# Projections in tiles of 32 columns, and one PSUM accumulator for both halves of an LSTM step

## The chip, the cores and the metric

The kernel runs on one core of one Trainium2 chip. The metric is the device time of one execution in microseconds (us). TensorE multiplies matrices and writes its results to PSUM; VectorE (DVE in the profile) and ScalarE (ACT) read them there. GpSimd (POOL) and SyncE (SP) issue loads and do a little preparation.

## The reference

Four residual layers run over x of shape (4, 1024, 512), each reading the sum so far. Cut to what matters:

```python
x = x + rnn(x)     # h = tanh(x_t @ Wx + b + h @ Wh)
x = x + ssm(x)     # conv of 4 taps, proj @ Wp, u = x @ Ws, a scan over time, y @ Wo + bo
x = x + lstm(x)    # A = x_t @ Wx + b + h @ Wh; i,f,o = sigmoid; g = tanh
                   # c = f*c + i*g; h = o*tanh(c)
x = x + adapt(x)   # x @ (base + rank-8 update), per batch row
```

The RNN and the LSTM are sequential: 1024 steps, each of which needs the h of the step before. Batch is 4, so a step multiplies only 4 rows of h by a 512 x 512 (RNN) or 512 x 2048 (LSTM) matrix.

## The kernel before

**Chunks and passes.** Time is cut into 32 chunks of 32 steps (slots). A pass `do_pass(c)` runs the LSTM on chunk c, the RNN on chunk c+2, the state-space layer for chunk c+1 and the adapter layer for chunk c-1, so that four layers are under way at once. Passes -2 and -1 are a prologue without LSTM; passes 1 to 24 are in a loop unrolled 12 times. Order on every engine is the order in which the program is written (`manual_schedule`); the framework puts in the semaphore waits. In a slot the order is: all LSTM matmuls; a job for TensorE, if the slot has one; the RNN matmuls; then the work of VectorE and ScalarE.

**A step of the LSTM.** h is held in float32 and split into three bf16 parts (`split`, line 203), so that 4 batch rows times 3 parts make 12 stationary columns. TensorE is used as four tiles of 32 columns (`CT = 32`): tile j takes the same 12 columns of h and a quarter of the outputs, and writes to PSUM partitions 32j and up. The outputs are worked on in two halves, A and B (`mh` = 0 and 1), 256 columns for each tile: 64 for each of four gates. Each half has its own accumulator, `acc2[0]` and `acc2[1]`, each in a PSUM bank of its own. The contraction runs over four chunks k of h; half A makes the chunks 0 and 1 of the new h, half B the chunks 2 and 3. A matmul at line 365 covers one k, one bf16 part of the weights, one tile and one half: 4 x 3 x 4 x 2 = 96 of 256 columns. They are ordered A (k = 0, 1), B (k = 0), A (k = 2, 3), B (k = 1, 2, 3), so that A's sums are complete after 60.

**What follows the matmuls.** `Half` holds it: `transpose` (line 382) reads the half's accumulator from PSUM, `sum` (387) adds the bf16 parts and the input projection, `gates` (394) is tanh on ScalarE, then `products` (398), `cell` (403), `tanh` (408), `h` (411) and two `split` (203). A and B are interleaved in an order written out by hand: A's transpose, A's sum, B's transpose, A's gates, A's products, and so on. `rnn_mm` (340), `rnn_pre` (348, 349) and `rnn_h` (352) are the RNN's step.

**Projections.** They are matrix products over a whole chunk (128 tokens), placed in slots by `jobs`: the taps of the state-space layer (437) in slots 1 to 4, `skip` (444) in slot 5, its output (493) in slot 13, and `project2` (329), the LSTM's input, in slots 15 to 30. These four use the array with 128, 64 or 128 stationary columns at once. `project0` (315), the RNN's input in slots 0 and 10 to 12, already runs as four tiles of 32. The adapter's matmuls (678) run in slots 6 to 9. Results of projections are moved out of PSUM at line 304. The tile `pb` holds the taps' result in `pb[:, 0]` and the skip result in `pb[:, 1]`, both in one bank; ScalarE reads the first at lines 461, 462 and 465.

**Loads.** `wx2` (4 MB) comes in four pieces through the buffer `xw2[0]`, and POOL copies each into its columns' order (line 173). `wo` comes in four DMAs.

Of the kernel before, what the change touches and what calls it, by code (L numbers as in the profile page):

```python
# [8 lines left out]
F32 = mybir.dt.float32  # L9
# [29 lines left out]
def cond_resid_kernel(ctx: ExitStack, tc: tile.TileContext, a: dict, out: bass.AP):  # L39
# [117 lines left out]
    wp = const.tile([P, TAPS, KC, 2 * NS], F32, name="wp", tag="wp")  # L157
    quads(nc.sync, wp[:, TAPS - 1], a["Wp"].rearrange("(j c q) n -> j q c n", j=4, c=KC))
    ws = load_rows(const, "ws", a["Ws"], NS, nc.sync)

    wo = const.tile([NS, D], F32, name="wo", tag="wo")
    for c in range(KC):
        nc.sync.dma_start(
            out=wo[:, P * c : P * (c + 1)].rearrange("p (j q) -> p j q", j=4),
            in_=a["Wo"].rearrange("p (j c q) -> p j c q", j=4, c=KC)[:, :, c],
        )
    wx2 = const.tile([P, KC, 4 * D], F32, name="wx2", tag="wx2")
    come = xw2[0].rearrange("p g c t b -> p (g c t b)")
    for k in range(KC):
        quads(nc.sync, come, a["Wx2"].rearrange("(j c q) n -> j q c n", j=4, c=KC)[:, :, k])  # L170
        for g in range(4):
            cols = slice(g * D, (g + 1) * D)
            nc.gpsimd.tensor_copy(
                wx2[:, k, cols].rearrange("p (c j q) -> p c j q", c=KC, j=4),
                come[:, cols].rearrange("p (j c q) -> p c j q", j=4, c=KC),
            )
    w1 = layer[:, 1]

    base = layer[:, B - 1]
# [17 lines left out]
    def upper(x):  # L197

        return x.bitcast(BF16)[..., 1::2]
# [17 lines left out]
    nc.vector.memset(s1, 0.0)  # L217

    acc0 = psum.tile([P, P], F32, name="acc0", tag="acc0")
    acc2 = [psum.tile([P, 2 * P], F32, name=f"acc2{i}", tag=f"acc2{i}") for i in range(2)]  # L220
    for t in (acc0, *acc2):
        nc.vector.memset(t, 0.0)

    def softplus_parts(dst, z, n, tag, cut=1):
# [75 lines left out]
    def bank(name, shape, tag="fill", bufs=2):  # L300
        return psum.tile(shape, F32, name=name, tag=tag, bufs=bufs)

    def evacuate(dst, ps, bias, scale):
        nc.scalar.activation(dst.rearrange("p t b -> p (t b)"), ps, AF.Identity, bias=bias, scale=scale)  # L304

    def project0(c, m):

        ps = bank("proj0", [P, TOK])

        def mm():  # L310

            for k in range(KC):
                for j in range(4):
                    n0 = P * j + CT * m
                    nc.tensor.matmul(  # L315
                        ps[CT * j : CT * (j + 1), :], wx0[:, k, n0 : n0 + CT], xin[c % XBUFS][:, k],
                        start=(k == 0), stop=(k == KC - 1),
                    )

        return mm, lambda: evacuate(xw0[c % 2][:, m], ps, b0[:, 0, m : m + 1], 1.0)  # L320

    def project2(c, g, m):

        ps = bank("proj2", [P, TOK])
        n0 = g * D + P * m

        def mm():
            for k in range(KC):
                nc.tensor.matmul(  # L329
                    ps, wx2[:, k, n0 : n0 + P], x2[c % 2][:, k], start=(k == 0), stop=(k == KC - 1)  # L330
                )

        return mm, lambda: evacuate(xw2[c % 2][:, g, m], ps, b2s[:, g, m : m + 1], 1.0 if g == 3 else 0.5)


    def rnn_mm(c, t):
# [15 lines left out]
        nc.scalar.activation(h0[c % 2][:, :, t, :], pre0[t % 2], AF.Tanh)  # L352


    def lstm_mm(c, t, kh, mh, ks=(0, 1)):


        h = h2[c % 2] if t else h2[(c - 1) % 2]
        for k in (2 * kh + x for x in ks):
            parts = upper(h[:, k, (t - 1) % TC].rearrange("p s b -> p (s b)"))  # L360
            for n in range(NP):
                w = wh2[n][:, k].rearrange("p (g n) -> p g n", g=4)
                for j in range(4):
                    n0 = P * j + 2 * CT * mh
                    nc.tensor.matmul(  # L365
                        acc2[mh][CT * j : CT * j + NP * B, :], parts, w[:, :, n0 : n0 + 2 * CT],
                        start=(k == 0 and n == 0), stop=(k == KC - 1 and n == NP - 1),
                    )

    def lstm_input(c, t, m):  # L370
        nc.scalar.copy(tt2[m][t % 2][:, :, :, :B], xw2[c % 2][:, :, 2 * m : 2 * m + 2, t, :])  # L371
# [1 line left out]
    class Half:  # L373
# [6 lines left out]

        def transpose(self):
            nc.vector.transpose(  # L382
                self.tt[:, :, :, B:].rearrange("p g c b -> p (g c) b"), acc2[self.m]
            )

        def sum(self):
# [34 lines left out]
    def ssm_jobs(c):  # L421
        x, h, po = xin[c % XBUFS], h0[c % 2], {}
        v, act = nc.vector, nc.scalar

        def sm(name):
            return small.tile([NS, TOK], F32, name=name, tag=name, bufs=1)

        jobs = [
            (m // 2, ("gap", "end")[m % 2], lambda m=m: v.tensor_add(x1[:, m, 3:, :], x[:, m], h[:, m]))
            for m in range(KC)  # L430
        ]
        pb = bank("pb", [P, 2, TOK], tag="pb", bufs=1)


        def taps(k):
            for tap in range(TAPS):
                nc.tensor.matmul(  # L437
                    pb[:, 0, :], wp[:, tap, k], x1[:, k, tap : tap + TC, :],
                    start=(tap == 0 and k == 0), stop=(tap == TAPS - 1 and k == KC - 1),
                )  # L440

        def skip():
            for k in range(KC):
                nc.tensor.matmul(  # L444
                    pb[:NS, 1, :], ws[:, k], x1[:, k, 3:, :], start=(k == 0), stop=(k == KC - 1)
                )

        cg, z, e, u, w, p = (sm(n) for n in ("cg", "z", "e", "u", "w", "p"))
        bt, vv, y = z, e, w
        v3, y3 = (t.rearrange("p (t b) -> p t b", b=B) for t in (vv, y))  # L450
        y_last = y3[:, TC - 1, :]
        jobs += [(1 + k, "pe", lambda k=k: taps(k)) for k in range(KC)]
        jobs.append((5, "pe", skip))

        def turn(n):
            cols = slice(n * TOK // 4, (n + 1) * TOK // 4)
            v.reciprocal(u[:, cols], u[:, cols])


        jobs += [  # L460
            (4, "end", lambda: act.activation(z, pb[:NS, 0, :], AF.Identity, bias=vec[:NS, 0:1])),
            (4, "end", lambda: act.activation(e, pb[:NS, 0, :], AF.Abs, bias=vec[:NS, 0:1])),
            (5, "end", lambda: act.activation(e, e, AF.Exp, scale=-1.0)),
            (5, "end", lambda: act.activation(u, e, AF.Copy, bias=2.0)),
            (6, "end", lambda: act.activation(cg, pb[NS:, 0, :], AF.Tanh, bias=vec[NS:, 0:1])),
            (7, "end", lambda: v.tensor_mul(u, u, e)),
            (7, "end", lambda: v.tensor_mul(w, u, u)),
            (7, "end", lambda: act.activation(p, w, AF.Copy, scale=2.0 * SERIES[-1])),
            (12, "end", lambda: act.copy(s1, y_last)),
        ]  # L470

        chain = [lambda q=q: v.scalar_tensor_tensor(p, p, 2.0 * q, w, ALU.add, ALU.mult) for q in SERIES[-2::-1]]
        chain += [
            lambda: v.scalar_tensor_tensor(p, p, 2.0, u, ALU.add, ALU.mult),
            lambda: v.scalar_tensor_tensor(bt, z, 0.0, p, ALU.max, ALU.add),
            lambda: v.scalar_tensor_tensor(vv, pb[:NS, 1, :], vec[:NS, 1:2], bt, ALU.add, ALU.mult),
        ]
        for b in range(B):
            chain.append(lambda b=b: v.tensor_tensor_scan(
                y3[:, :, b], decay, v3[:, :, b], s1[:, b : b + 1], ALU.mult, ALU.add  # L480
            ))

        chain += [
            lambda: v.scalar_tensor_tensor(y, y, dt, cg, ALU.mult, ALU.mult),
        ]
        place = lambda n: ("gap", "end", "end")[n % 3]
        jobs += [(6 + n // 3, place(n), lambda n=n: turn(n)) for n in range(4)]
        jobs += [(8 + n // 3, place(n), f) for n, f in enumerate(chain)]

        def out_mm():  # L490
            po[0] = bank("ssm_out", [P, KC, TOK], tag="po", bufs=1)
            for m in range(KC):
                nc.tensor.matmul(po[0][:, m, :], wo[:, P * m : P * (m + 1)], y, start=True, stop=True)  # L493

        def x2_end(m):
            v.scalar_tensor_tensor(
                x2[c % 2][:, m].rearrange("p t b -> p (t b)"), po[0][:, m, :], bo[:, 0, m : m + 1],
                x1[:, m, 3:, :].rearrange("p t b -> p (t b)"), ALU.add, ALU.add,
            )

        jobs += [
            (13, "pe", out_mm),
            *((13 + m // 2, "end", lambda m=m: x2_end(m)) for m in range(KC)),
            (14, "end", lambda: act.copy(x1[:, :, 0:3, :], x1[:, :, TC : TC + 3, :])),
        ]
        return jobs
# [187 lines left out]
    def do_pass(c, src=None, dst=None, lstm=True, rnn=True, ssm=True, last=False):  # L694
# [23 lines left out]
        for t in range(TC):  # L718
            if lstm:
                A, Bh = Half(c, t, 0), Half(c, t, 1)  # L720
                lstm_mm(c, t, 0, 0)
                lstm_mm(c, t, 0, 1, (0,))
                lstm_mm(c, t, 1, 0)
                lstm_mm(c, t, 0, 1, (1,))
                lstm_mm(c, t, 1, 1)
            do(t, "pe")
            if rnn:
                rnn_mm(c + 2, t)
# [119 lines left out]
```

## Time and profile before

| What | Value |
|---|---|
| Median of 3 runs | 5007.96 us (5005.07 to 5009.45) |
| Profiled execution, its own time | 5000.53 us |
| Its span | 4998.8 us, TensorE clock 0.987 of full |
| TensorE matmuls busy | 4776.3 us, 96% |
| VectorE busy | 3728.2 us, 75% |
| L365, LSTM matmuls | 98304, 2877.8 us busy |
| L340, RNN matmuls | 32768, 1106.6 us busy |
| L329, `project2` matmuls | 4096, 593.3 us busy |
| L315, `project0` matmuls | 4096, 137.2 us busy |
| L382, LSTM transposes on VectorE | 2048 of 450 ns |

A float32 matmul appears as two records, so counts at L329 and L315 are twice those of the program. PE is TensorE's matmul, PEld its weight load, which overlaps. A line of a group reads: line, engine, operation, out<-in by name, shapes, count | busy us, mean ns of one | idle time of the engine before it and what ended it. In the timeline a line has its start, its duration and, in brackets, the idle time of that engine before it. Busy time counts overlapping matmuls once.

### The profile page before, as it was taken

The page shows a single profiled execution, that of the slowest core. Times are in us where ns is not written, and L with a number is a line of the kernel's source. Part 1 is how long each engine was busy: PE and PEld are TensorE (multiplying, and loading weights), DVE is VectorE, ACT ScalarE, POOL GpSimd, SP SyncE. Part 2 cuts the span into 40 slices and gives each one's busy share as a digit, 9 for nine tenths or more (in the row PEclk, how much of TensorE's full clock was granted, in tenths as well). Part 3 has the DMA queues.
Part 4 walks back from the last instruction along what each step waited for, and adds up shares of the span by engine and source line. Part 5 has one row for each costly group of instructions (what it writes and reads, how often), then busy time and mean ns, then how long its engine had stood idle before and what let it go on. Part 6 is the DMA issues. An engine that isn't in the chain of part 4 may idle for free.

```text
span 4998.8 us, 313167 instructions
## 1 busy us (share of the span) xinstructions
PE 4776.3 (96%) x142944; PEld 4156.1 (83%) x142944; DVE 3728.2 (75%) x17652; ACT 1617.2 (32%) x8135; POOL 62.9 (1%) x110
## 2 busy tenths in 40 slices
PE   5899999999999999999999999999999999999976
PEld 3778888888888888888888888888888888888864
DVE  3577777777777777777777777777777777777766
ACT  2223333333333333333333333333333333333322
POOL 3000000000000000000000000000000000000000
PEclk6999999999999999999999999999999999999999
DMA  5210000000000000000000000000000000000000
GB/s 130 92 38 8 8 6 8 6 8 8 8 8 6 6 8 8 8 9 6 8 6 9 8 9 8 6 6 8 9 8 8 6 7 7 8 6 6 4 5 7
DMA packets 39957, 66.97 MB, mean 13 GB/s; under 512 B 10321, under 2 KB 27345, under 8 KB 37601
## 3 DMA queue, kind: packets, MB, share of 16 engines
q1 hardware_dynamic: 34688, 45.64, 3.5%
q8 instruction: 1119, 18.33, 1.5%
q10 hardware_dynamic: 1728, 1.06, 0.1%
q14 instruction: 214, 1.75, 0.1%
q0 software_dynamic: 2208, 0.19, 0.0%
HBM read 38.34 MB, written 8.39 MB: 9 GB/s over the span
## 4 chain that ended last, share of the span: by engine, by line
PE 53%; DVE 3%; issue 0%; ACT 0%; DVEq 0%
PE acc L365 33%; PE acc L340 10%; PE proj L329 6%; PE pb L437 1%; PE ada L678 1%; PE proj L315 1%; DVE tt L382 1%; DVE gc L387 1%; DVE h L203 1%; PE ssm_out L493 0%; DVE prod L398 0%; DVE h L411 0%; PE pb L444 0%; DVE gc L403 0%; ACT x L685 0%
## 5 line engine op out<-in xcount | busy, mean ns | idle before, releaser
L365 PE MATMUL acc<-wh,h 128*12 128x256 bf16 x98304 | 2877.8, 273 | 132.2 <-DVE h L203 124.3
L365 PEld LDWEIGHTS <-h 128*12 128x12 bf16 x98304 | 2511.0, 88 | 369.4 <-DVE h L203 211.5
L382 DVE STREAM_TRANSPOSE tt<-acc 128x256 f32<-128x256 f32 x2048 | 920.6, 450 | 667.0 <-PE acc L365 544.4
L340 PE MATMUL acc<-wh,h 128*4 128x128 f32 x32768 | 1106.6, 277 | 49.2 <-ACT h L352 47.4
L340 PEld LDWEIGHTS acc<-wh,h 128*4 128x4 f32 x32768 | 794.1, 87 | 261.5 <-ACT h L352 62.7
L394 ACT ACTIVATE gc<-gc 128x32 f32<-128x32 f32 x2048 | 469.6, 229 | 1323.1 <-DVE gc L387 1242.5
L387 DVE TENSOR_REDUCE gc<-tt 128x32 f32<-128x128 f32 x2048 | 766.9, 374 | 35.3
L203 DVE TENSOR_TENSOR h<-h 128x8 f32<-128x8 f32 (+1 forms) x4098 | 681.4, 166 | 104.6
L408 ACT ACTIVATE th<-gc 128x8 f32<-128x8 f32 x2048 | 427.2, 209 | 828.8 <-DVE gc L403 828.8
L352 ACT ACTIVATE h<-pre 128x16 f32<-128x16 f32 x1024 | 221.2, 216 | 1179.4 <-DVE pre L349 1179.4
L329 PE MATMUL proj<-x,wx 128*128 128x128 f32 x4096 | 593.3, 288 | 6.9 <-ACT xw L304 6.7
L329 PEld LDWEIGHTS proj<-x,wx 128*128 128x128 f32 x4096 | 495.6, 191 | 119.6 <-issue 110.6
L411 DVE SCALAR_TENSOR_TENSOR h<-gc,th 128x8 f32<-128x8 f32 x2048 | 342.1, 167 | 221.7 <-ACT th L408 204.6
L348 DVE STREAM_TRANSPOSE tt<-acc 128x128 f32<-128x128 f32 x1024 | 315.7, 308 | 76.6 <-PE acc L340 76.4
L403 DVE SCALAR_TENSOR_TENSOR gc<-prod 128x8 f32<-128x8 f32 x2048 | 341.5, 167 | 35.5
L371 ACT COPY tt<-xw 128x32 f32<-128x32 f32 x2048 | 327.8, 207 | 0.0
L398 DVE SCALAR_TENSOR_TENSOR prod<-gc 128x16 f32<-128x16 f32 x2048 | 314.8, 154 | 0.0
L349 DVE TENSOR_TENSOR pre<-xw,tt 128x16 f32<-128x16 f32 x1024 | 180.6, 176 | 37.7 <-DVE tt L348 0.5
L304 ACT ACTIVATE xw<-proj,b2s 128x128 f32<-128x128 f32 x512 | 179.4, 350 | 0.0
L315 PE MATMUL proj<-xin,wx 128*32 128x128 f32 x4096 | 137.2, 277 | 17.2 <-DMA wh<-in_Wh_dram 16.2
L437 PE MATMUL pb<-x,wp 128*128 128x128 f32 x1024 | 149.1, 289 | 0.0
L437 PEld LDWEIGHTS pb<-x,wp 128*128 128x128 f32 x1024 | 124.7, 192 | 28.0 <-issue 27.8
(114 smaller groups left out, 1095.7 us busy)
## 6 DMA issues: line engine op xcount, KB each, us to landing
layer<-in_w2T_dram SPq DMA_DIRECT2D x32, 512.0 KB, 3.6
xin<-in_xT_dram SPq DMA_DIRECT2D x128, 64.0 KB, 2.2
out_dram<-x SPq DMA_DIRECT2D x128, 64.0 KB, 1.8
layer<-in_Wh_dram SPq DMA_DIRECT2D x16, 256.0 KB, 10.3
xw<-in_Wx_dram SPq DMA_DIRECT2D x16, 256.0 KB, 4.3
wx<-in_Wx_dram SPq DMA_DIRECT2D x4, 256.0 KB, 5.1
wh<-in_Wh_dram ACTq DMA_DIRECT2D x4, 256.0 KB, 6.4
layer<-in_w_dram SPq DMA_DIRECT2D x4, 256.0 KB, 7.3
```

Of the source, the lines that this page charges most:

```text
L203: nc.vector.tensor_tensor(h[:, :, n], h[:, :, n - 1], upper(h[:, :, n - 1]), ALU.subtract)
L329: nc.tensor.matmul(ps, wx2[:, k, n0 : n0 + P], x2[c % 2][:, k], start=(k == 0), stop=(k == KC - 1))
L340: nc.tensor.matmul(acc0[CT * j : CT * j + B, :], h[:, k, (t - 1) % TC, :], wh0[:, k, j * P : (j + 1) * P], start=(k == 0), stop=(k == KC - 1),
L365: nc.tensor.matmul(acc2[mh][CT * j : CT * j + NP * B, :], parts, w[:, :, n0 : n0 + 2 * CT], start=(k == 0 and n == 0), stop=(k == KC - 1 a ...
L371: nc.scalar.copy(tt2[m][t % 2][:, :, :, :B], xw2[c % 2][:, :, 2 * m : 2 * m + 2, t, :])
L382: nc.vector.transpose(self.tt[:, :, :, B:].rearrange("p g c b -> p (g c) b"), acc2[self.m])
L387: nc.vector.tensor_reduce(self.gc[:, :4].rearrange("p g c b -> p (g c) b"), self.tt[:, :, :, : (1 + NP) * B].rearrange("p g c (s b) -> p ( ...
L394: nc.scalar.activation(self.gc[:, :4], self.gc[:, :4], AF.Tanh)
L403: nc.vector.scalar_tensor_tensor(self.c, self.prod[:, 1], 0.5, self.prod[:, 0], ALU.mult, ALU.add)
L408: nc.scalar.activation(self.th, self.c, AF.Tanh, scale=0.5)
L411: nc.vector.scalar_tensor_tensor(self.out[:, :, 0], self.gc[:, 2], 1.0, self.th, ALU.add, ALU.mult)
L437: nc.tensor.matmul(pb[:, 0, :], wp[:, tap, k], x1[:, k, tap : tap + TC, :], start=(tap == 0 and k == 0), stop=(tap == TAPS - 1 and k == KC ...
```

## The change

Three things change. The projections at lines 437, 444, 329 and 493 are issued in tiles of 32 columns through a helper `tiled`, as `project0` already was; `project0` and `project2` share one function. The two LSTM accumulators become one tile `acc2` of [128, 2, 256] float32[...]. For chunk k = 0 of h the matmuls cover both halves at once, 12 of 512 columns in place of 24 of 256; the order is then A (k = 1), A (k = 2, 3), B (k = 1), B (k = 2, 3), in matmuls of 256 columns as before. The work of VectorE and ScalarE keeps its order. Since `project2` now picks 32 columns per tile, `wx2` is loaded in its own layout with four DMAs and no copies, and `wo` with one.

```diff
-    wo = const.tile([NS, D], F32, name="wo", tag="wo")
-    for c in range(KC):
-        nc.sync.dma_start(
...
-    come = xw2[0].rearrange("p g c t b -> p (g c t b)")
-    for k in range(KC):
-        quads(nc.sync, come, a["Wx2"].rearrange("(j c q) n -> j q c n", j=4, c=KC)[:, :, k])
-        for g in range(4):
-            cols = slice(g * D, (g + 1) * D)
-            nc.gpsimd.tensor_copy(
...
+    wo = load(const, "wo", [NS, D], a["Wo"], nc.sync)
+    wx2 = load_rows(const, "wx2", a["Wx2"], 4 * D, nc.sync)
...
-    acc2 = [psum.tile([P, 2 * P], F32, name=f"acc2{i}", tag=f"acc2{i}") for i in range(2)]
-    for t in (acc0, *acc2):
+    acc2 = psum.tile([P, 2, 2 * P], F32, name="acc2", tag="acc2")
+    for t in (acc0, acc2):
...
+    def tiled(dst, columns, x, first=True, final=True, tiles=4):
+
+        for j in range(tiles):
+            nc.tensor.matmul(dst[CT * j : CT * (j + 1)], columns(j), x, start=first, stop=final)
+
+    def project(dst, w, x, c0, bias, scale):
+
+
+        ps = bank("proj", [P, TOK])
 
         def mm():
             for k in range(KC):
-                nc.tensor.matmul(
-                    ps, wx2[:, k, n0 : n0 + P], x2[c % 2][:, k], start=(k == 0), stop=(k == KC - 1)
-                )
...
+                tiled(ps, lambda j: w[:, k, c0 + P * j : c0 + P * j + CT], x[:, k], k == 0, k == KC - 1)
...
-    def lstm_mm(c, t, kh, mh, ks=(0, 1)):
-
+    def lstm_mm(c, t, k, m0, m1):
 
         h = h2[c % 2] if t else h2[(c - 1) % 2]
...
+        parts = upper(h[:, k, (t - 1) % TC].rearrange("p s b -> p (s b)"))
+        for n in range(NP):
+            w = wh2[n][:, k].rearrange("p (g j m n) -> p j m g n", g=4, j=4, m=2)
+            for j in range(4):
+                dst = acc2[CT * j : CT * j + NP * B, m0 : m1 + 1].rearrange("p m (g n) -> p m g n", g=4)
+                if m0 == m1:
+                    dst, src = dst[:, 0], w[:, j, m0]
+                else:
+                    src = w[:, j]
+                nc.tensor.matmul(
+                    dst, parts, src, start=(k == 0 and n == 0), stop=(m1 == 1 and k == KC - 1 and n == NP - 1),
+                )
...
-                self.tt[:, :, :, B:].rearrange("p g c b -> p (g c) b"), acc2[self.m]
+                self.tt[:, :, :, B:].rearrange("p g c b -> p (g c) b"), acc2[:, self.m]
...
-                nc.tensor.matmul(
-                    pb[:, 0, :], wp[:, tap, k], x1[:, k, tap : tap + TC, :],
-                    start=(tap == 0 and k == 0), stop=(tap == TAPS - 1 and k == KC - 1),
+                tiled(
+                    pb[:, 0, :], lambda j: wp[:, tap, k, CT * j : CT * (j + 1)], x1[:, k, tap : tap + TC, :],
+                    tap == 0 and k == 0, tap == TAPS - 1 and k == KC - 1,
                 )
...
-                nc.tensor.matmul(
-                    pb[:NS, 1, :], ws[:, k], x1[:, k, 3:, :], start=(k == 0), stop=(k == KC - 1)
+                tiled(
+                    pb[:, 1, :], lambda j: ws[:, k, CT * j : CT * (j + 1)], x1[:, k, 3:, :],
+                    k == 0, k == KC - 1, tiles=NS // CT,
                 )
...
-                nc.tensor.matmul(po[0][:, m, :], wo[:, P * m : P * (m + 1)], y, start=True, stop=True)
+                tiled(po[0][:, m, :], lambda j: wo[:, P * j + CT * m : P * j + CT * (m + 1)], y)
...
-                lstm_mm(c, t, 0, 0)
-                lstm_mm(c, t, 0, 1, (0,))
-                lstm_mm(c, t, 1, 0)
-                lstm_mm(c, t, 0, 1, (1,))
-                lstm_mm(c, t, 1, 1)
+
+                lstm_mm(c, t, 0, 0, 1)
+                lstm_mm(c, t, 1, 0, 0)
+                for m in range(2):
+                    if m:
+                        lstm_mm(c, t, 1, 1, 1)
+                    for k in (2, 3):
+                        lstm_mm(c, t, k, m, m)
```

More of the change, by code (lines that the diff above doesn't have):

```diff
@@ L159, in cond_resid_kernel @@
     ws = load_rows(const, "ws", a["Ws"], NS, nc.sync)
-    wo = const.tile([NS, D], F32, name="wo", tag="wo")
-    for c in range(KC):
-        nc.sync.dma_start(
-            out=wo[:, P * c : P * (c + 1)].rearrange("p (j q) -> p j q", j=4),
-            in_=a["Wo"].rearrange("p (j c q) -> p j c q", j=4, c=KC)[:, :, c],
-        )
-    wx2 = const.tile([P, KC, 4 * D], F32, name="wx2", tag="wx2")
-    come = xw2[0].rearrange("p g c t b -> p (g c t b)")
-    for k in range(KC):
-        quads(nc.sync, come, a["Wx2"].rearrange("(j c q) n -> j q c n", j=4, c=KC)[:, :, k])
-        for g in range(4):
-            cols = slice(g * D, (g + 1) * D)
-            nc.gpsimd.tensor_copy(
-                wx2[:, k, cols].rearrange("p (c j q) -> p c j q", c=KC, j=4),
-                come[:, cols].rearrange("p (j c q) -> p c j q", j=4, c=KC),
-            )
+    wo = load(const, "wo", [NS, D], a["Wo"], nc.sync)
+    wx2 = load_rows(const, "wx2", a["Wx2"], 4 * D, nc.sync)
     w1 = layer[:, 1]
@@ L301, in bank, with end, project0 @@
         return psum.tile(shape, F32, name=name, tag=tag, bufs=bufs)
[L303 to L308, printed above, removed]
+    def tiled(dst, columns, x, first=True, final=True, tiles=4):
[3 more added lines that the diff above has]
+        ps = bank("proj", [P, TOK])
         def mm():
             for k in range(KC):
-                for j in range(4):
-                    n0 = P * j + CT * m
-                    nc.tensor.matmul(
[L316 to L320, printed above, removed]
-    def project2(c, g, m):
[L324 to L328, printed above, removed]
-                nc.tensor.matmul(
-                    ps, wx2[:, k, n0 : n0 + P], x2[c % 2][:, k], start=(k == 0), stop=(k == KC - 1)
-                )
-        return mm, lambda: evacuate(xw2[c % 2][:, g, m], ps, b2s[:, g, m : m + 1], 1.0 if g == 3 else 0.5)
+                tiled(ps, lambda j: w[:, k, c0 + P * j : c0 + P * j + CT], x[:, k], k == 0, k == KC - 1)
+        def end():
+            nc.scalar.activation(dst.rearrange("p t b -> p (t b)"), ps, AF.Identity, bias=bias, scale=scale)
+        return mm, end
+    def project0(c, m):
+        return project(xw0[c % 2][:, m], wx0, xin[c % XBUFS], CT * m, b0[:, 0, m : m + 1], 1.0)
+    def project2(c, g, m):
+        return project(
+            xw2[c % 2][:, g, m], wx2, x2[c % 2], g * D + CT * m, b2s[:, g, m : m + 1], 1.0 if g == 3 else 0.5
+        )
     def rnn_mm(c, t):
@@ L352, in rnn_h @@
         nc.scalar.activation(h0[c % 2][:, :, t, :], pre0[t % 2], AF.Tanh)
-    def lstm_mm(c, t, kh, mh, ks=(0, 1)):
+    def lstm_mm(c, t, k, m0, m1):
         h = h2[c % 2] if t else h2[(c - 1) % 2]
[L359 to L368, printed above, removed]
+        parts = upper(h[:, k, (t - 1) % TC].rearrange("p s b -> p (s b)"))
[9 more added lines that the diff above has]
+                    dst, parts, src, start=(k == 0 and n == 0), stop=(m1 == 1 and k == KC - 1 and n == NP - 1),
+                )
     def lstm_input(c, t, m):
@@ L436, in taps @@
             for tap in range(TAPS):
-                nc.tensor.matmul(
-                    pb[:, 0, :], wp[:, tap, k], x1[:, k, tap : tap + TC, :],
-                    start=(tap == 0 and k == 0), stop=(tap == TAPS - 1 and k == KC - 1),
+                tiled(
+                    pb[:, 0, :], lambda j: wp[:, tap, k, CT * j : CT * (j + 1)], x1[:, k, tap : tap + TC, :],
+                    tap == 0 and k == 0, tap == TAPS - 1 and k == KC - 1,
                 )
@@ L443, in skip @@
             for k in range(KC):
-                nc.tensor.matmul(
-                    pb[:NS, 1, :], ws[:, k], x1[:, k, 3:, :], start=(k == 0), stop=(k == KC - 1)
+                tiled(
+                    pb[:, 1, :], lambda j: ws[:, k, CT * j : CT * (j + 1)], x1[:, k, 3:, :],
+                    k == 0, k == KC - 1, tiles=NS // CT,
                 )
```

## The prediction

> **What bounds the kernel now.** I read the page's busy table first, then its costliest groups, then the waits, then single steps in the timeline. The busy table says TensorE:
>
> ```profile
> PE 4776.3 (96%) x142944; PEld 4156.1 (83%) x142944; DVE 3728.2 (75%) x17652; ACT 1617.2 (32%) x8135; POOL 62.9 (1%) x110
> ```
>
> That is a mean. The waits (waiter <- releaser: us in total, times, longest) show a second limit beside it:
>
> ```profile
> DVE tt L382 <- PE acc L365: 544.4, 799, 4.9
> PEld L365 <- DVE h L203: 211.5, 353, 2.0
> ```
>
> VectorE's transposes wait for the LSTM's matmuls, and in 353 of 1024 steps the next LSTM matmuls wait for the h that VectorE makes (L203 splits it into bf16 parts). So there are two kinds of step, and the timeline (start, duration, engine, line) tells them apart. First one with a projection beside it:
>
> ```profile
> 2643.19 2.80 PE L365 MATMUL acc<-wh,h 128*12 128x256 bf16 x96
> ...
> 2645.05 0.45 DVE L382 STREAM_TRANSPOSE tt<-acc 128x256 f32<-128x256 f32 x1 [0.47 <-PE acc L365]
> 2645.54 0.38 DVE L387 TENSOR_REDUCE gc<-tt 128x32 f32<-128x128 f32 x1
> 2645.92 0.97 PEld L437 LDWEIGHTS pb<-x,wp 128*128 128x128 f32 x8 [0.22 <-issue]
> 2645.92 1.16 PE L437 MATMUL pb<-x,wp 128*128 128x128 f32 x8
> 2645.95 0.23 ACT L394 ACTIVATE gc<-gc 128x32 f32<-128x32 f32 x1 [1.42 <-DVE gc L387]
> 2646.03 0.45 DVE L382 STREAM_TRANSPOSE tt<-acc 128x256 f32<-128x256 f32 x1
> ```
>
> The transpose of half A starts 1.86 us after the first LSTM matmul, though the 96 matmuls run for 2.80 us: it **reads A's accumulator while TensorE still fills B's**. B's transpose starts at 2.84 us. TensorE is never idle; the next transpose of A comes at 2649.75, so this step takes 4.70 us. Then a step of the last chunk, where TensorE has nothing but the LSTM:
>
> ```profile
> 4960.56 2.80 PE L365 MATMUL acc<-wh,h 128*12 128x256 bf16 x96 [1.65 <-DVE h L203]
> ...
> 4962.43 0.45 DVE L382 STREAM_TRANSPOSE tt<-acc 128x256 f32<-128x256 f32 x1 [0.97 <-PE acc L365]
> 4962.91 0.37 DVE L387 TENSOR_REDUCE gc<-tt 128x32 f32<-128x128 f32 x1
> 4963.32 0.23 ACT L394 ACTIVATE gc<-gc 128x32 f32<-128x32 f32 x1 [2.46 <-DVE gc L387]
> 4963.41 0.45 DVE L382 STREAM_TRANSPOSE tt<-acc 128x256 f32<-128x256 f32 x1
> 4963.78 0.13 DVE L398 SCALAR_TENSOR_TENSOR prod<-gc 128x16 f32<-128x16 f32 x1
> ...
> 4965.02 2.51 PEld L365 LDWEIGHTS <-h 128*12 128x12 bf16 x96 [1.95 <-DVE h L203]
> ```
>
> Here the loop through h sets the step: 1.87 us to A's transpose, 2.59 us from it to the next LSTM matmul, 4.46 us together (4.45 from start to start). By the starts of L365, 22 of a chunk's 32 steps take about 4.69 us (slots 1 to 5, 13 and 15 to 30, where a projection of more than 32 columns runs) and 10 take 4.45 us; even the projections already in four tiles (L315, slots 10 to 12) fit inside 4.45. So **TensorE bounds 22 steps, and only by 0.24 us; the h loop stands right behind**.
>
> The last lines decide the forecast. In the second half of the prologue, slot 5 writes the skip projection (L444) into `pb[:, 1]`, just after ScalarE read `pb[:, 0]`, other columns of the same PSUM bank:
>
> ```profile
> 150.76 0.35 ACT L461 ACTIVATE z<-pb,vec 64x128 f32<-64x128 f32 x1
> 151.01 0.35 ACT L462 ACTIVATE e<-pb,vec 64x128 f32<-64x128 f32 x1
> 151.41 0.85 PEld L444 LDWEIGHTS pb<-x,ws 128*64 128x64 f32 x8 [1.12 <-ACT e L462]
> 151.42 1.09 PE L444 MATMUL pb<-x,ws 128*64 128x128 f32 x8 [0.89 <-ACT e L462]
> ```
>
> L444 reads only `ws` and `x1`, nothing ScalarE makes at L462, yet TensorE stood idle for 0.89 us and started 0.06 us after L462 ended. The only thing shared is the bank of `pb`. So this program's waits go by bank, not by the columns touched.
>
> [...] In the first step above, from L365's start to L437's start 96 matmuls took 2.73 us, 28.4 ns each and 114 ns per group of four tiles[...].
>
> **The change, part by part.**
>
> 1. *One accumulator tile.* Both halves, 2 x 256 f32, fill one tile, so one bank. A's transpose comes after all LSTM matmuls in program order. If waits go by bank, it **waits for B's last matmul**: at 2.80 us less part 2, plus 0.04 for the wait. Instead of 1.86 that is 2.82 us. Queued behind it on VectorE are both sums, the products, the cells, h and its splits; ScalarE's gates wait for the sum, and TensorE's next LSTM matmuls for the splits.
>
> 2. *512 columns.* 24 matmuls of 256 become 12 of 512 (chunk k=0 for both halves). [...] Three groups fewer: -0.02 us. Bounds: 0, and -0.05 if the 12 weight loads saved count too. The read pattern keeps its runs of 64, so I expect no loss; the upper end is +0.05.
>
> 3. *The chain after A's transpose.* It was 2.59 us to the next matmul. In it B's transpose had to wait for TensorE: A's sum ended 0.85 after A's transpose began, B's transpose began at 0.98. Now it follows A's sum directly. A's products came 0.37 after B's transpose began; now at 0.85 + 0.37 = 1.22, or at 1.15 if VectorE overlaps the starts (gates end at 1.12), instead of 1.35. Gain 0.13 to 0.20, taken as 0.16: 2.43 us.
>
> So **a step is 2.82 + 2.43 = 5.25 us**, in every slot.
>
> 4. *Does TensorE still bind?* No. The LSTM takes 2.71 start to start, the RNN 0.87 (L340's start to the next L365's), a tiled projection 0.88 (the RNN starts 3.50 us after the LSTM in slot 10, with one, and 2.62 in slot 14, with none; a wide one makes it 3.82): 4.46 of 5.25. h of half B comes 0.95 us after h of half A (ends of the L203 splits), as before; TensorE needs it after three groups of 220 ns and three of 114, 1.00 us.
>
> 5. *Projections in tiles of 32.* L329, L437, L444 and L493 go from 8 matmul records of 145 ns (593.3/4096) to 32 like L315 (137.2/4096 = 33.5 ns). TensorE gains 0.2 to 0.3 us in 22 steps[...]. Under part 1 this is worth nothing: it adds to an idle stretch. Were that cover gone it would be worth the 0.24 us. Four times the weight loads (L315's: 116.3/4096 = 28 ns each) stay inside the 0.88.
>
> 6. *The load of Wx2 and Wo.* 16 DMAs of 256 KB through `xw2[0]`, each set waiting for POOL, plus 16 POOL copies (11.1 us busy, 40.5 us waiting, done by 85 us) become 4 DMAs of 1 MB; four of `wo` become one. SP's waits for L173 (19.3 us) go. All land well before 140 us, when `wx2` is first near; the prologue is paced there by the RNN's loop. Taken as 0; bounds -5 and +10 us. Tiled projections in pass -1: -3.
>
> **Sum**, against the profiled execution (5000.53 us; span 4998.8). Chunks 1 to 29: 22 x (5.25 - 4.69) + 10 x (5.25 - 4.45) = 20.3 us each, 589. Chunks 30 and 31 are all 4.45: 64 x 0.80 = 51. Chunk 0 averages 5.76 because adapter work queues behind the RNN; I take +0.4 per step, 13 (bounds 0 and 26). Last step +1, prologue -3. Together +651: 5651. The median of the runs shown is 7.4 us above the profiled one: **5658 us**.
>
> **Rivals.**
>
> *No wait by bank* (waits follow columns, or the accumulator takes two banks): the other side. L444 speaks against it, though it shows a write waiting for a read, not a read waiting for a write. Then A's transpose stays at about 1.85, the h loop at 4.44 and TensorE at 4.46, so all slots run at about 4.45: chunks 1 to 29 lose 22 x 0.24 = 5.3 us each, 153, the rest some 10: **4845 us**. It decides where A's transpose starts before about 2.2 us: with the 2.43 of part 3 the h loop then stays under today's mean step, 4.62 us; later than that the kernel is slower.
>
> *The wait, and a slower clock*: TensorE's idle stretches grow, in chunk 31 from 1.65 to about 2.5 us per step. The trace shows the granted clock at 0.50 in the prologue (82 to 104 us), with TensorE 66% busy and gaps of 0.96 us. Against it: between 4845 and 4985 us the clock held 1.00 at the same 66%. At half clock chunk 31 costs 32 x 2.7 = 86 us more: **5744 us**.
>
> *The chain eats less or more than in part 3*: 5.15 or 5.35 a step, **5555 or 5760 us**.
>
> Chances: wait by bank at full clock 0.83, with a slow stretch 0.07, no wait 0.08, something that cancels to no change 0.02. The range 5530 to 5780 takes in the bounds of parts 2 and 3 (0.1 us on 1023 steps, 100 us each way) and the slower clock. No change means within 0.2%, about what a measurement of this kernel can tell. Faster 0.08, same 0.02, slower 0.90.
>
> **What would show it.** Right: A's transpose begins at 2.8 us, B's follows A's sum with no wait; L382's wait for L365 grows from 544 to about 1400 us (0.9 more per step); L365 waits for L203 about 1 us in nearly every step; TensorE's share falls to about 80%; RNN starts come at 3.5 us or before in all slots. Wrong: A's transpose still at 1.9 us, or wide-projection and bare steps of different length.

## The result, and the profile after

The changed kernel takes 5718.5 us (median of 4 runs, 5714.9 to 5721.1) against 5006.5 for the kernel before: ratio 1.142, 95% interval 1.140 to 1.144. The profiled execution took 5716.2 us, its span is 5714.4.

The busy table and the two groups of the page that answer to those of before (group: busy us, mean ns | idle time before it and what ended it):

```profile
PE 4731.1 (83%) x147040; PEld 3563.2 (62%) x147040; DVE 3695.3 (65%) x17651; ACT 1616.6 (28%) x8135; POOL 50.2 (1%) x94
...
L347 PE MATMUL acc<-wh,h 128*12 128x256 bf16 (+1 forms) x86016 | 2910.9, 291 | 890.2 <-DVE h L188 878.9
...
L363 DVE STREAM_TRANSPOSE tt<-acc 128x256 f32<-128x256 f32 x2048 | 908.0, 443 | 1418.9 <-PE acc L347 1418.5
```

TensorE is busy for 45 us less than before, yet its share fell from 96% to 83%: the work did not grow, the waiting did. L347 is the old L365, L363 the old L382, L188 the old L203. The waits of the changed kernel (waiter <- releaser: us in total, times, longest) name both ends of the loop:

```profile
DVE tt L363 <- PE acc L347: 1418.5, 1015, 9.1
...
PE acc L347 <- DVE h L188: 878.9, 1008, 2.6
```

VectorE now waits for the LSTM's matmuls 1015 times, 1418.5 us in all (before: 799 times, 544.4 us), and TensorE waits for h 1008 times, 878.9 us in all (before: 129 times, 124.3 us). One step, in a slot with a projection in four tiles, in the timeline (of the 84 matmuls at L347, 12 are 512 columns wide and 72 are 256):

```profile
2504.78 2.79 PE L347 MATMUL acc<-wh,h 128*12 128x512 bf16 x84 [0.74 <-DVE h L188]
...
2507.40 1.05 PE L291 MATMUL proj<-xin,wx 128*32 128x128 f32 x32
2507.62 0.45 DVE L363 STREAM_TRANSPOSE tt<-acc 128x256 f32<-128x256 f32 x1 [0.94 <-PE acc L347]
2508.11 0.39 DVE L368 TENSOR_REDUCE gc<-tt 128x32 f32<-128x128 f32 x1
2508.16 0.86 PEld L320 LDWEIGHTS acc<-wh,h 128*4 128x4 f32 x32
2508.27 1.05 PE L320 MATMUL acc<-wh,h 128*4 128x128 f32 x32
2508.42 0.44 DVE L363 STREAM_TRANSPOSE tt<-acc 128x256 f32<-128x256 f32 x1
...
2510.07 1.95 PEld L347 LDWEIGHTS <-h 128*12 128x12 bf16 x64 [1.04 <-DVE h L188]
```

A's transpose starts 2.84 us after the first LSTM matmul (1.86 before), at the end of the stream of 2.79. B's transpose follows A's sum with no wait in brackets, 0.80 us after A's began. From A's transpose to the next LSTM matmul it is 2.45 us here, and 2.44 in the middle of all steps. By the starts of the LSTM matmuls in the trace, nearly every slot takes 5.27 to 5.29 us, with or without a projection; an ordinary chunk takes 168.9 us against 147.7.

The last chunk is longer again. A step of it, and then the window that covers the last chunk and a little before (length; busy us of TensorE, weight loads, VectorE, ScalarE and GpSimd; granted clock; DMA share and GB/s):

```profile
5674.69 4.35 PE L347 MATMUL acc<-wh,h 128*12 128x512 bf16 x84 [2.48 <-DVE h L188]
...
5679.10 0.45 DVE L363 STREAM_TRANSPOSE tt<-acc 128x256 f32<-128x256 f32 x1 [3.51 <-PE acc L347]
```

```profile
5480.00:5700.00 220.00, 140.79 (x2920) 84.52 (x2920) 98.26 (x479) 38.33 (x207) 0.00 (x0) 0.80 0.01 3
```

The same 84 matmuls took 4.35 us in place of 2.79, after an idle stretch of 2.48 us, and the mean granted clock of the window is 0.80 of full. The 31 intervals between this chunk's 32 steps add up to 203.3 us; at 5.27 they would be 163.4. In 25 of them a step takes 6.8 to 6.9 us. Those of slots 7 to 11 still take 5.26 or 5.27: the adapter's matmuls, in slots 6 to 9, leave TensorE only 1.62 us idle before the LSTM's next ones, and the clock from 5535 to 5565 us is 1.00.

### The profile page after: what moved, and what is told of

The parts are those of the page before. It is cut to its first block, busy times and chain, and to the rows that moved or that the text cites. A ratio compares the mean times of both kernels' runs of the same rounds, so it can differ in the third digit from the quotient of the medians.

```text
span 5714.4 us, 321312 instructions
## 1 busy us (share of the span) xinstructions
PE 4731.1 (83%) x147040; PEld 3563.2 (62%) x147040; DVE 3695.3 (65%) x17651; ACT 1616.6 (28%) x8135; POOL 50.2 (1%) x94
## 3 DMA queue, kind: packets, MB, share of 16 engines
q8 instruction: 1151, 18.86, 1.4%
## 4 chain that ended last, share of the span: by engine, by line
PE 31%; DVE 25%; issue 1%; ACT 0%; DVEq 0%
PE acc L347 31%; DVE tt L363 9%; DVE gc L368 7%; DVE h L188 3%; DVE prod L379 3%; DVE h L392 2%; DVE gc L384 2%; PE ada L660 0%; ACT x L667 0%; ACT th L389 0%; DVEq L829 0%; DVE tt L328 0%; ACT h L332 0%; DVE pre L329 0%
## 5 line engine op out<-in xcount | busy, mean ns | idle before, releaser
L347 PE MATMUL acc<-wh,h 128*12 128x256 bf16 (+1 forms) x86016 | 2910.9, 291 | 890.2 <-DVE h L188 878.9
L347 PEld LDWEIGHTS <-h 128*12 128x12 bf16 x86016 | 1972.4, 88 | 1837.8 <-DVE h L188 1176.4
L363 DVE STREAM_TRANSPOSE tt<-acc 128x256 f32<-128x256 f32 x2048 | 908.0, 443 | 1418.9 <-PE acc L347 1418.5
L320 PEld LDWEIGHTS acc<-wh,h 128*4 128x4 f32 x32768 | 807.1, 88 | 233.6 <-issue 81.8
L188 DVE TENSOR_TENSOR h<-h 128x8 f32<-128x8 f32 (+1 forms) x4098 | 682.9, 167 | 104.7
L291 PE MATMUL proj<-x,wx 128*32 128x128 f32 x16384 | 537.0, 273 | 5.8 <-ACT xw L303 5.4
L291 PEld LDWEIGHTS proj<-x,wx 128*32 128x32 f32 x16384 | 452.4, 110 | 13.5 <-ACT xw L303 7.0
L379 DVE SCALAR_TENSOR_TENSOR prod<-gc 128x16 f32<-128x16 f32 x2048 | 358.7, 175 | 0.0
L660 PE MATMUL ada<-layer,x 128*32 128x512 f32 x1024 | 134.2, 603 | 3.8 <-DVE x L653 3.8
L291 PE MATMUL pb<-x,wp 128*32 128x128 f32 x4096 | 135.0, 274 | 0.0
```

Source lines behind the costliest of these rows:

```text
L188: nc.vector.tensor_tensor(h[:, :, n], h[:, :, n - 1], upper(h[:, :, n - 1]), ALU.subtract)
L291: nc.tensor.matmul(dst[CT * j : CT * (j + 1)], columns(j), x, start=first, stop=final)
L320: nc.tensor.matmul(acc0[CT * j : CT * j + B, :], h[:, k, (t - 1) % TC, :], wh0[:, k, j * P : (j + 1) * P], start=(k == 0), stop=(k == KC - 1),
L347: nc.tensor.matmul(dst, parts, src, start=(k == 0 and n == 0), stop=(m1 == 1 and k == KC - 1 and n == NP - 1),)
L363: nc.vector.transpose(self.tt[:, :, :, B:].rearrange("p g c b -> p (g c) b"), acc2[:, self.m])
L379: nc.vector.scalar_tensor_tensor(self.prod, self.gc[:, 0:2], 1.0, self.gc[:, 3:5], ALU.add, ALU.mult)
```

## Experiments

My theory going in: the one accumulator, in one bank, makes A's transpose wait for B's matmuls; nothing else in the change costs anything. The rival: the wider matmuls or the tiled projections carry the loss themselves.

### Two accumulators again, projections still tiled

```diff
-    acc2 = psum.tile([P, 2, 2 * P], F32, name="acc2", tag="acc2")
+    acc2 = [psum.tile([P, 2 * P], F32, name=f"acc2{i}", tag=f"acc2{i}") for i in range(2)]
...
-                lstm_mm(c, t, 0, 0, 1)
-                lstm_mm(c, t, 1, 0, 0)
...
+                lstm_mm(c, t, 0, 0)
+                lstm_mm(c, t, 0, 1, (0,))
...
```

> The projections in tiles of 32 and the new loads stay; the LSTM has its two accumulators and 96 matmuls of 256 columns again. Theory (the shared bank makes A's transpose wait for B's matmuls): A's transpose starts at 1.86 us of a step again and, with the wide projections gone, every slot takes about 4.45 us: 4845 us (4830 to 4870), faster than the kernel before. Rival (the tiled projections cost something on their own, by four times the weight loads): the wide slots stay at 4.69 us or more, 5007 us or above.

Measured: 4944.4 us (4929.4 to 4950.7), ratio to the kernel before 0.987, interval 0.985 to 0.989. The sign is the theory's and the loss is gone. VectorE's wait for the LSTM's matmuls is back to 498.7 us, and where nothing else disturbs, A's transpose starts at 1.87 us of the step:

```profile
DVE tt L362 <- PE acc L345: 498.7, 885, 5.9
...
2523.58 2.80 PE L345 MATMUL acc<-wh,h 128*12 128x256 bf16 x96 [0.78 <-DVE h L188]
...
2525.45 0.45 DVE L362 STREAM_TRANSPOSE tt<-acc 128x256 f32<-128x256 f32 x1
```

But the size is off by 100 us. Slots 6 to 11 and 15 to 16 take 4.46 us, slots 18 to 30 average 4.64, and ordinary chunks differ by some 4 us. The timeline shows what is in the way (here inside the RNN's matmuls, one such place of many):

```profile
2757.87 0.48 PE L320 MATMUL acc<-wh,h 128*4 128x128 f32 x6
...
2758.64 0.64 PEld L320 LDWEIGHTS acc<-wh,h 128*4 128x4 f32 x25 [0.57 <-issue]
2758.64 0.93 PE L320 MATMUL acc<-wh,h 128*4 128x128 f32 x25 [0.28 <-issue]
```

TensorE stops in the middle of a run of 32 like matmuls, waiting for nothing that the profile shows. Such gaps often lie exactly 256 TensorE records apart (four in a row between 2754 and 2767 us). More on this in the last experiment.

### One tile, but two banks

```diff
-    acc2 = psum.tile([P, 2, 2 * P], F32, name="acc2", tag="acc2")
+    acc2 = psum.tile([P, 2, 4 * P], F32, name="acc2", tag="acc2")
...
-acc2[:, self.m]
+acc2[:, self.m, : 2 * P]
```

The matmuls are the 96 of 256 columns, and write `acc2[..., mh, : 2 * P]`. Each half has its own start and stop flags again. A and B now begin 2 KB apart in a row of the tile, as much as the whole tile had that the prediction counts as one bank; by that count each half lies in another bank. No view of the profile shows the banks.

> As the kernel with two accumulators and tiled projections, but the accumulator is one tile of two banks, half A in the first bank and half B in the second. Theory (waits go by bank): the same time as with two accumulators, within 10 us, about 4845. Rival (waits go by tile): A's transpose starts at 2.84 us and the time is that of the changed kernel or a little more, 5715 to 5745.

Measured: 5731.6 us, ratio 1.145 (1.144 to 1.147). The rival is right, and my reading of the wait falls. The waits, and a step in the timeline (its first LSTM matmul starts at 2502.56):

```profile
DVE tt L362 <- PE acc L345: 1435.4, 1015, 8.6
...
2505.40 0.45 DVE L362 STREAM_TRANSPOSE tt<-acc 128x256 f32<-128x256 f32 x1 [1.00 <-PE acc L345]
...
2506.18 0.44 DVE L362 STREAM_TRANSPOSE tt<-acc 128x256 f32<-128x256 f32 x1
```

A's transpose waits for B's matmuls, to 2.84 us of the step, although they go, by the count above, to another bank and end with a stop flag of their own; B's again has no wait. That both halves belong to **one tile** is enough for the wait, which the framework puts in: with two tiles the same matmuls and transposes overlap. Two tiles in one bank were not tried, so whether a shared bank alone would bring it too is not known.

### The kernel before with only the accumulators merged

```diff
-    acc2 = [psum.tile([P, 2 * P], F32, name=f"acc2{i}", tag=f"acc2{i}") for i in range(2)]
+    acc2 = psum.tile([P, 2, 2 * P], F32, name="acc2", tag="acc2")
...
-                        start=(k == 0 and n == 0), stop=(k == KC - 1 and n == NP - 1),
+                        start=(mh == 0 and k == 0 and n == 0), stop=(mh == 1 and k == KC - 1 and n == NP - 1),
```

> The kernel before with one edit: both accumulators in one tile of one bank, still 96 matmuls of 256 columns, wide projections, old loads. Theory: the whole loss appears from this edit alone, every slot takes about 5.27 us and wide projections are hidden in the idle stretch: 5725 us (5700 to 5745), the same as the changed kernel within 20 us. Rival (the matmuls of 512 columns or the tiled projections carry the loss): near 5007 us.

Measured: 5734.6 us, ratio 1.146 (1.144 to 1.147). This edit alone makes the whole loss:

```profile
DVE tt L382 <- PE acc L365: 1430.6, 1015, 9.2
```

Its wide slots (RNN start at 3.81 us of the step) and its bare ones (2.62) both take 5.28 us, so the wide projections are hidden too.

### The changed kernel with 256 columns, and with 512 everywhere

```diff
-                lstm_mm(c, t, 0, 0, 1)
-                lstm_mm(c, t, 1, 0, 0)
...
+                for k in range(KC):
+                    lstm_mm(c, t, k, 0, 1)
```

(The diff is that of 512 everywhere: 48 matmuls a step. The other kernel has the 96 matmuls of before, in one tile.)

> The changed kernel with chunk k = 0 in 24 matmuls of 256 columns in place of 12 of 512; one bank. As predicted, 512 columns saved 0.02 us a step, so this is 20 us slower than the changed kernel: 5738 us. Other answer (wider matmuls save nothing, since A's transpose came at 2.84 and not 2.82 us): 5718 us within 5.

> The changed kernel with every chunk k in matmuls of 512 columns: 48 for a step in place of 84; one accumulator tile, so nothing is lost by finishing both halves together. As predicted (7 ns saved per group of four that is merged, 9 more groups): 0.063 us less a step, 64 us: 5654 us. Other answer (the changed kernel's chunks took 168.88 us against 169.13 with 256 columns, 8 ns a step for 3 groups): 9 groups save 24 ns a step, 5694 us.

Measured: 5733.4 us with 256 everywhere, between the two answers, and 5692.2 with 512 everywhere, the second one; the changed kernel has 5718.5. An ordinary chunk takes 169.13, 168.88 and 168.13 us with 0, 3 and 12 merged groups of four tiles. The saving is 8 ns a step for the first three groups and 23 for the next nine, 2.6 ns per group in both, against the 7 that I had estimated (0.02 us for three groups in part 2); no trace showed that figure. The rest of the 15 us between 256 and the changed kernel is mostly in chunk 30 (179.0 against 170.2 us in the profiled runs), next to the slow stretch; with the other one-tile accumulators this chunk took 173 to 178. The kernel with 256 differs from the merged kernel before by 1.2 us, with all four projections tiled in one and wide in the other, and an ordinary chunk takes 169.13 us tiled and 169.00 wide: under the wait, tiling them is worth nothing.

### Work added to keep the clock up

```diff
-            if rnn:
+            if rnn or lstm:
                 rnn_mm(c + 2, t)
```

> The changed kernel with the RNN's matmuls going on in the last two passes, their results never read: work added. Theory (idle stretches of 2.5 us lower TensorE's clock in chunk 31, whose steps took 203 us in place of 169): with TensorE busy the clock stays up, chunk 31 takes 169 us, and the kernel gets about 35 us faster by doing more: 5683 us. Rival (the long steps have another cause, or the added matmuls cost their own time): 5718 us or more.

Measured: 5670.4 us (5669.6 to 5671.8): 48 us faster than the changed kernel, with 2048 more records of matmuls. The window of its last chunk:

```profile
5480.00:5660.00 180.00, 128.16 (x3965) 91.72 (x3957) 100.24 (x484) 38.08 (x204) 0.00 (x0) 1.00 0.02 5
```

The clock is 1.00, and the 31 intervals take 163.5 us. The added matmuls lie in TensorE's idle stretch and cost nothing. In this chunk the slower clock that came with the idle stretch had cost 40 us; the rest of the 48 is in small differences elsewhere.

### Fewer tiled projections, two accumulators

The page's busy table and DMA table together show what a gap 256 records apart can be. TensorE of the kernel with two accumulators and all projections tiled has 159328 matmuls and as many weight loads; the first queue of instruction DMAs (queue, kind: packets, MB, share):

```profile
PE 4678.1 (95%) x159328; PEld 3911.6 (79%) x159328; DVE 3738.5 (76%) x17652; ACT 1617.0 (33%) x8135; POOL 50.2 (1%) x94
```

```profile
q8 instruction: 1247, 20.43, 1.7%
```

318656 records in blocks of 256 are 1244.75; the queue moved 1247 packets of 16.4 KB (20.43 MB/1247). In the kernel before it is 1116.75 and 1119, in the changed kernel 1148.75 and 1151: always 2.25 more. From these three counts I take it that this queue brings TensorE's instructions (a matmul and a weight load are one each), 256 to a packet. The gaps also keep step with the queue. Between 300 and 4700 us of this run, TensorE's stream pauses 236 times for more than 0.25 us from one record's start to the next without a wait; four in five of these pauses end 1.28 to 1.59 us after a packet of the queue has landed, where moments taken at random lie 0.39 to 3.40 us after one.

```diff
+                cuts = [(0, P)] if m == 3 else [(CT * j, CT) for j in range(4)]
+                for at, n in cuts:
                     nc.tensor.matmul(
-                        ps, wx2[:, k, n0 : n0 + P], x2[c % 2][:, k], start=(k == 0), stop=(k == KC - 1)
+                        ps[at : at + n], wx2[:, k, n0 + at : n0 + at + n], x2[c % 2][:, k], ...
```

The taps in the same way, with `k == 3`; for the second run, `m % 2` and `k % 2`. Both start from the kernel before.

> The kernel before with its two accumulators and its loads; of the wide projections, 12 of the 16 of project2 and 3 of the 4 of the taps run in four tiles of 32, the others wide, skip and output wide. With all of them tiled, slots 18 to 30 took 4.63 us and not 4.45: gaps of 0.2 to 1.0 us in TensorE's stream, often 256 TensorE instructions apart. Theory (the instruction stream can't be supplied at 320 records per 4.45 us for long; it gives about 68 a us): at 308 records per 4.51 us it just holds, 12 slots at 4.45 and 4 at 4.69, 50 us less than with all tiled: 4895 us (4880 to 4915). Rival (the gaps belong to the tiled projections themselves, whatever the rate): the tiled slots stay at 4.63 and the wide ones at 4.69, 4945 to 4975 us.

> As the kernel before, but every second wide projection (odd m of project2, odd k of the taps) stays wide and the others run in tiles of 32: 296 TensorE records per 4.57 us on average, 65 a us, against 58 in the kernel before (no gaps), 67 with three in four tiled (4.60 us on average in slots 15 to 30) and 69 with all (4.62). Theory (the supply of instructions falls behind above some rate): few gaps 256 records apart, slots 15 to 30 average 4.57 to 4.59 us, 4905 to 4930 us. Rival (the tiled projections bring their gaps with them at any rate): the tiled slots average 4.55 or more and the wide ones 4.69, 4935 to 4960 us.

Measured: 4934.5 us with three in four tiled (ratio 0.985, 0.984 to 0.987), a miss of the 4895 that I expected; 4932.3 with every second one (0.985, 0.984 to 0.987), 2 us above the range given. With every second one the picture is clean: slots 15 to 30 take 4.45 and 4.69 us in turn, to within 0.01. At 65 TensorE records a us the gaps are gone: pauses as above add up to 15 us over the run, as against 12 in the kernel before, 47 with three in four tiled and 116 with all. With three in four tiled, the third tiled slot of a group takes 4.49 to 4.62 us on average and the wide one after it 4.75 to 4.89; with all tiled, slots 18 to 30 take 4.64. So the gaps come where many records are used up in a row, not with the tiled projections as such: a single tiled slot or two in a row run at 4.45 to 4.51. That it is the supply of TensorE's instructions that lags is my reading of the packets and the pauses. There is no plain cap, as I had assumed with 68 a us: the two denser kernels average 67 and 69 with gaps. On that reading, how far ahead the supply runs, and why it lags by up to 1 us at a time, stays open.

## Why the prediction was right, and where it was wrong

**The direction and the path** were right: A's transpose behind B's last matmul, the chain of h behind that, TensorE idle, wide and bare slots alike. Merging the accumulators alone gives the loss, and separating them takes it away.

**The reason for the wait was wrong in one word.** The prediction read from L444 that "waits go by bank, not by the columns touched". L444 and L462 share a bank, but they also share the tile `pb`, and the trace of before could not tell these apart. One tile over two banks waits just the same: waits by bank gave about 4845 us for it, and it took 5731.6. That the forecast came out right all the same is luck in this one point: the change puts both halves into one tile and one bank at once, so either reading gives the same number. The step that named "the accumulator takes two banks" as a way out of the wait fails with it: two tiles are the way out (here each in a bank of its own).

**The sum.** Profile against profile the loss is 715.6 us, predicted 651.

- Chunks 1 to 29: 614, predicted 589. The step is 5.277 us and not 5.25. A's transpose came at 2.84 us, not 2.82, mostly since part 2 counted on an estimate of 7 ns per merged group and 2.6 were to be had. Part 3 was right to 0.01 us (2.44 against 2.43).
- Chunks 30 and 31: 93, predicted 51. This is the rival with the slower clock, which I gave 0.07. I priced it at 86 us for a whole chunk at half clock; it cost 40. The argument against it, that the last chunk held full clock at 66% busy before, was too weak: what had changed was the length of one idle stretch in each step, from 1.65 to 2.48 us. The run with RNN matmuls added, which fill that stretch, bears this out: 1.00 in place of 0.80. No idle stretch in this chunk or the one before is longer than 2.5 us; stretches of 2.48 us that come back every step were enough.
- Chunk 0: 11, predicted 13. Before the first LSTM matmul: -6, predicted -3 (the loads and the tiled projections were rightly near nothing). After the last: +3, predicted +1.

**Part 2's saving** of 0.02 us, 7 ns for each of three groups, was an estimate. It starts from 114 ns per group, read in a step with a wide projection after the LSTM. In a step with a tiled one after it (slot 12), 2.63 us lie between the two starts, not 2.73, or 110 ns per group; the other 0.10 us came with the wide projection:

```profile
2536.20 2.80 PE L365 MATMUL acc<-wh,h 128*12 128x256 bf16 x96
...
2538.83 1.05 PE L315 MATMUL proj<-xin,wx 128*32 128x128 f32 x32
...
2539.70 1.05 PE L340 MATMUL acc<-wh,h 128*4 128x128 f32 x32
```

Groups of four start 109 ns apart all through that trace (median), and merged ones of 512 columns 217 apart in the changed kernel. That leaves 1 or 2 ns for a merged group, near the 2.6 of the chunk times and far from 7.

**Under the wait, tiling is worth nothing**: right, 1.2 us between the two kernels that differ in it.

**The rival without the wait** was mis-sized: 4845 us, measured 4944. It took TensorE's need, 4.46 us in part 4, for the tiled slot's length in every slot. That sum counts 2.71 us for the LSTM, again with a wide projection after it, and not 2.63; with the RNN's start at 3.50 us in slot 10 it is 3.50 + 0.87 = 4.37, so the loop through h (4.45) should have set the slot. Neither allows for the gaps in TensorE's stream. In the trace of before only three tiled slots stood in a row (10 to 12), and those ran at 4.45; sixteen in a row brought the gaps, and slots 18 to 30 took 4.64. Part 5's price, 0.24 us for each of 22 slots once the cover is gone, holds for slots that take turns with wide ones.

**A version that beats both**: two accumulators with every second wide projection tiled, 4932.3 us, 1.5% faster than the kernel before. That with three in four tiled is as fast within the intervals, and that with all tiled nearly so.

## What to carry to other kernels

If two engines are to overlap on two halves of an accumulator, give each half its own tile, in a bank of its own as here: with one tile, the reader of the first half waited for the last writer of the second (to 2.84 us of the step, 1.87 with two tiles), even where the halves lay 2 KB apart. Before merging matmuls to save overhead, ask what the merged operand ties together: here 8 ns a step were saved and 0.66 us lost. When a cost is read from the time to the next instruction, look at what that next instruction is: it may bring a cost of its own. And where one engine gets idle stretches that it did not have, look at its clock in the window where they are longest.

## What the runs showed of the hardware

- TensorE's clock fell with regular short idle stretches: where most steps had one of 2.48 us (changed kernel, 5480 to 5700 us), its mean was 0.80. With 1.65 us (before, 4845 to 4985 us), 1.62 us (changed kernel, 5535 to 5565 us) and 0.74 us (changed kernel, 2500 to 2550 us) it was 1.00. Added matmuls that nobody reads brought 1.00 again and took 40 us off that chunk.
- TensorE's stream paused when it was dense: at an average of 65 records (matmuls and weight loads) a us in slots 15 to 30 the pauses without a wait added up to 15 us over the run, at 67 to 47 us, at 69 to 116 us; in the kernel before, at 58, to 12 us. Three slots in a row at 72 still took 4.45 us each in the kernel before (slots 10 to 12, after slots with fewer records).
- Four tiles of 32 columns finish a float32 projection of 128 columns in 0.88 us where one wide matmul sequence takes 1.19, by the shift of the RNN's start (2.62 us of the step with none, 3.50 and 3.81 with one).
- Groups of four column tiles started 109 ns apart with 256 bf16 columns and 217 apart with 512 (medians): merging two saved 2.6 ns by the chunk times.
